# Cross-attention with a state-space layer: projections cut into pieces, maxima over two steps, sums on ScalarE, keys and values fetched per unit

## The chip, the cores and the metric

The kernel runs on one core of a Trainium2 chip, in float32. A core has five engines with queues of their own: TensorE (PE in the profile; its weight loads are shown apart as PEld), VectorE (DVE), ScalarE (ACT), GpSimd (POOL) and SyncE (SP, which here only issues transfers). Each works through its queue in order, and an instruction that waits holds up all that is behind it. PE writes to PSUM, a small memory of eight banks; DVE and ACT read it from there. The metric is the time on the device in microseconds; the median of runs is compared.

## The reference, cut to what matters

Of 4096 rows of width 512, each is normalized and attends to 3202 context rows with eight heads of 64; then follow a projection with a residual, a second normalization, a linear recurrence with a SiLU in it, and an output:

```python
x1  = x + mha(layernorm(x, g1, b1), layernorm(ctx, g1, b1))   # softmax(q k^T / 8) v, then W_o
u   = (layernorm(x1, g2, b2) @ W_in.T + b_in) @ Bmat          # 4096 x 64
s_t = silu(s_{t-1} @ A.T) + u_t                               # over 4096 positions
out = x1 + states @ Cmat + mean(program_probs) @ W_prog.T + b_prog
```

## The kernel before

There are three stages. The **preparation** normalizes the context, projects it to keys and values in 13 double chunks of 246 to 248 context rows, and stores them to DRAM (kd, vd). A list of side work (`side`, which ends with `queries(0, x0)`) is advanced between its chunks. The **attention loop** takes the rows in eight query blocks Q of 512. A block has eight units: four pairs of heads (hp) times two halves of 256 rows. A unit has 13 steps, one for each double chunk of keys. The **tail** finishes the last block's four tiles and runs the recurrence in sweeps (L831), writing the output.

In the loop the order on every engine is written out by hand, step by step (L718 to L768). The steps of one unit overlap with those of the next: in step g PE computes the scores of step g (L459), ACT copies them from PSUM to SBUF (L469), DVE keeps a running elementwise maximum (L480, one step later), and once a unit's scores are all there (16 steps after each), DVE subtracts the row maximum (L514), ACT takes the exponential (L524) and POOL adds the weights up (L533), and PE multiplies with the values (L542). The scores have two PSUM buffers of two banks each. The row maximum of a unit comes from `maximum`: PE transposes the running maximum (tt, L491), DVE reduces it (L498), PE spreads it over the keys (mb, L506).

Everything else is background work, held in generators that are advanced between the steps. `finish` ends a unit: the product is copied, POOL folds the sums of weights (L588), PE transposes them (pd, L594), DVE adds them up and takes the reciprocal (L599, L600), ACT widens it (L602), PE transposes it (rb, L607), DVE scales the result (L613). `project` ends a block, for each of its four tiles of 128 rows: PE's projection (pa, L627), DVE's residual (L636), the second normalization (`normalize`: statistics on DVE, L111 and L113, three small operations on POOL, L115 to L119, the scaling on ACT, L125), transposes (tp, L136), their copy (L652), the product pu (L659) and u (L663). `queries` prepares the next block: normalization, transposes, projection pq (L175), and ACT's bias (L184). In `background` (L704) two lists take turns: `first` holds the finishing of units, `rest` projections and queries. A generator says at each yield whether the next part needs PE results (True), and up to two parts of a list are advanced in a step. A whole projection of a tile, eight matrix instructions of 512 columns (float32 takes two instructions for one multiplication), is one such part:

```python
            for c in range(NC):
                nc.tensor.matmul(pa, o_t[Q, c][:, t * P : (t + 1) * P], wo[:, c, :], ...)
            yield True
```

The background shares two PSUM banks (`ps_m`), the maxima among them. Keys and values are fetched four steps ahead, on SP's queue, once for both halves of a pair (`load_k`, `load_v`, 13 buffers each); SP's queue also carries the fetches of x and the stores of x1. Outside the hand-written parts (the tail) a planner orders the instructions.

Of the kernel before, what the change touches and what calls it, by code (L numbers as in the profile page):

```python
# [18 lines left out]
P = 128  # L19
# [26 lines left out]
def xattn_ssm_kernel(  # L46
# [58 lines left out]
    ln = actx.enter_context(tc.tile_pool(name="ln", bufs=2))  # L105
# [25 lines left out]

    def transposes(pool, tag, xh, n, name):

        tp = pool.tile([P, NC, P], F32, tag=tag, name=f"tp_{name}")
        for c in range(NC):
            nc.tensor.transpose(  # L136
                tp[:, c, :n], xh[:n, c * P : (c + 1) * P], ident[:n, :n]
            )
        return tp[:, :, :n]

    xp_ = actx.enter_context(tc.tile_pool(name="xp", bufs=2))
    xnp = actx.enter_context(tc.tile_pool(name="xnp", bufs=2))
    qp = actx.enter_context(tc.tile_pool(name="qp", bufs=6))
    ps_m = actx.enter_context(tc.tile_pool(name="ps_m", bufs=2, space=PSUM))
    qt = {}

    def queries(Q, fetched=None):

        xns = []
        for half in range(2):  # L150
            xn = xnp.tile([P, NC, QU], F32, tag="xn", name=f"xn_{Q}_{half}")
            xns.append(xn)
            for t in range(NT // 2):
                r = Q * QB + half * QU + t * P
                if fetched:
                    xt = fetched[:, half * (NT // 2) + t, :]
                else:
                    xt = xp_.tile([P, H], F32, tag="x", name=f"x_{r}", bufs=3)
                    nc.sync.dma_start(xt, x[r : r + P, :])
                    yield False  # L160
                scaled = normalize(xt, P, f"x{r}", later=True)
                yield False
                yield False
                xh = scaled()
                yield False
                tp = transposes(ps_m, "m", xh, P, f"x{r}")
                yield True
                nc.scalar.copy(xn[:, :, t * P : (t + 1) * P], tp)
                yield False
                yield False  # L170
        for hp in range(NC):
            pq = ps_m.tile([P, 512], F32, tag="m", name=f"pq_{Q}_{hp}")
            for half in range(2):
                for i in range(NC):
                    nc.tensor.matmul(  # L175
                        pq[:, half * QU : (half + 1) * QU],
                        wq[:, i, hp * P : (hp + 1) * P],
                        xns[half][:, i, :],
                        start=(i == 0),
                        stop=(i == NC - 1),  # L180
                    )
            yield True
# [5 lines left out]
            yield False  # L188
# [22 lines left out]
    def shift(k):  # L211

        pr = ps_m.tile([P, 512], F32, tag="m", name=f"pr_{k}")
# [9 lines left out]
        pb = ps_m.tile([P, 512], F32, tag="m", name=f"pb_{k}")  # L223
# [15 lines left out]
    def side():  # L239
# [30 lines left out]
        pw = ps_m.tile([P, 512], F32, tag="m", name="pw")  # L270
# [8 lines left out]
        pt = ps_m.tile([P, NC, P], F32, tag="m", name="pt")  # L279
# [12 lines left out]
        pb = ps_m.tile([P, 512], F32, tag="m", name="pb")  # L292
# [16 lines left out]
        pm = ps_m.tile([P, 512], F32, tag="m", name="pm")  # L309
# [11 lines left out]
        for dst, terms in (  # L321
# [3 lines left out]
            pr = ps_m.tile([P, 512], F32, tag="m", name="pr")  # L325
# [126 lines left out]
    def scores(w, c):  # L452
# [3 lines left out]
        for b in range(2):  # L456
            for a in range(2):
# [3 lines left out]
                    kts[(*w["at"][:2], c)][r, b * n : (b + 1) * n],  # L461
# [20 lines left out]
    def maximum(w):  # L482

        m = small.tile([P, 2, 2], F32, tag="m", name=f"m_{w['name']}")
        tps = []
        for t in range(2):
            tp = ps_m.tile([P, 2, 2, CK], F32, tag="m", name=f"tt_{w['name']}_{t}")
            tps.append(tp)
# [7 lines left out]
        yield  # L496
        for t in range(2):
            nc.vector.tensor_reduce(  # L498
                m[:, t, :], tps[t].rearrange("p a b k -> p a (b k)"), AX.X, ALU.max
            )  # L500
        yield
        mb = ps_b.tile([P, 2, QU], F32, tag="b", name=f"mb_{w['name']}")
        w["mb"] = mb
        for t in range(2):
            for a in range(2):
# [4 lines left out]
                )  # L510

# [23 lines left out]
    def product(w, c):  # L535
# [4 lines left out]
        for b in range(2):  # L540
            for a in range(2):
                nc.tensor.matmul(  # L542
                    w["po"][a * HD : (a + 1) * HD, 0, :],
                    vts[(*w["at"][:2], c)][:n, b, a * HD : (a + 1) * HD],
# [34 lines left out]

# [388 lines left out]
```

## Time and profile before

| | us |
|---|---|
| median of 3 runs (2635.56 to 2644.17) | 2643.56 |
| profiled execution, its own time | 2643.8 |
| its span, first to last instruction | 2642.0 |
| preparation | 0 to 263 |
| attention loop | 263 to 2498 |
| tail | 2498 to 2642 |

| engine | busy us | share of the span | instructions |
|---|---|---|---|
| PE | 2498.9 | 95% | 16588 |
| PEld | 1422.2 | 54% | 16588 |
| DVE | 2144.1 | 81% | 2320 |
| ACT | 1837.8 | 70% | 2085 |
| POOL | 2066.3 | 78% | 1170 |

Rows of the profile name line, engine, operation, output<-input and count, then busy time in us, the mean of one in ns, and the idle time before them with what ended it. The ends of matrix instructions are modelled, so a busy PE need not be at its peak; starts are recorded, and the distance from one start to the next is the safer reading. The granted clock of TensorE is full in the loop (1.00) and lower in the tail (0.68).

### The profile page before, as it was taken

Reading aid. Unit: us, or ns where it says so; the run is one execution under the profiler, and the core shown is the slowest. Engines: PE = TensorE matmul, PEld = TensorE weight load, DVE = VectorE, ACT = ScalarE, POOL = GpSimd, SP = SyncE. Lnnn points to the kernel's source line nnn. Section 1 sums busy time; section 2 is a strip of 40 time slices with the busy share of each in tenths; the row PEclk is TensorE's granted clock in tenths of the full one; section 3 lists DMA queues with packets and bytes.
Section 4 is the critical chain, followed back from the end, with each engine's and each line's share of the span. In section 5 each row is a group of like instructions: output and inputs, shape, how many; then the busy total and the mean of one; then the engine's idle time right before and its main releaser. Section 6 shows DMA issues by size and latency. Waiting matters only on the chain.

```text
span 2642.0 us, 44166 instructions
## 1 busy us (share of the span) xinstructions
PE 2498.9 (95%) x16588; PEld 1422.2 (54%) x16588; DVE 2144.1 (81%) x2320; ACT 1837.8 (70%) x2085; POOL 2066.3 (78%) x1170
## 2 busy tenths in 40 slices
PE   7989899999999999999999999999999999999857
PEld 3445456555565555555655555555655555555433
DVE  2210897999979897999799988999799979999725
ACT  2232787877878787878787777778787878788510
POOL 1020497998979997999799988989799979999860
PEclk9999999999999999999999999999999999999966
DMA  3422221112212121222112211222121312221133
GB/s 124 138 87 73 74 68 49 51 57 84 59 45 62 50 83 32 58 65 68 45 54 68 67 56 51 57 84 59 43 62 49 86 30 60 64 58 54 60 112 128
DMA packets 164458, 176.62 MB, mean 67 GB/s; under 512 B 13480, under 2 KB 137424, under 8 KB 164242
## 3 DMA queue, kind: packets, MB, share of 16 engines
q1 hardware_dynamic: 155070, 157.68, 20.6%
q10 hardware_dynamic: 9172, 16.06, 1.8%
q8 instruction: 134, 2.20, 0.4%
q14 instruction: 82, 0.67, 0.1%
HBM read 143.81 MB, written 29.89 MB: 66 GB/s over the span
## 4 chain that ended last, share of the span: by engine, by line
PE 50%; DVE 27%; issue 11%; ACT 7%; POOL 2%; DMA 1%; SPq 1%; ACTq 0%; DVEq 0%; POOLq 0%
DVE top L480 17%; PE s L459 14%; PE po L542 12%; DVE p L514 5%; PE pq L175 4%; ACT p L469 4%; PE pa L627 4%; PE pv L388 3%; PE pk L414 3%; ACT p L524 2%; PE tt L491 2%; PE py_c L870 1%; DVE rd L599 1%; PE mb L506 1%; PE pu L659 1%
## 5 line engine op out<-in xcount | busy, mean ns | idle before, releaser
L533 POOL TENSOR_TENSOR acc<-p,acc 123x1024 f32<-123x1024 f32 x698 | 1658.7, 2376 | 112.2 <-ACT p L524 70.6
L469 ACT COPY p<-s 123x1024 f32<-123x1024 f32 (+1 forms) x832 | 834.9, 1004 | 274.6 <-PE s L459 261.9
L514 DVE TENSOR_TENSOR p<-p,mb 123x1024 f32<-123x1024 f32 (+1 forms) x832 | 1000.0, 1209 | 0.8 <-PE mb L506 0.8
L459 PE MATMUL s<-q,k 64*123 64x256 f32 (+1 forms) x6656 | 941.4, 402 | 61.2 <-DVE top L480 49.4
L524 ACT ACTIVATE p<-p 123x1024 f32<-123x1024 f32 (+1 forms) x832 | 880.2, 1058 | 141.2 <-DVE p L514 134.0
L480 DVE TENSOR_TENSOR top<-s,top 123x1024 f32<-123x1024 f32 x704 | 855.9, 1216 | 140.1 <-ACT p L469 132.2
L542 PE MATMUL po<-p,v 123*64 123x256 f32 (+1 forms) x6656 | 900.4, 392 | 1.1 <-ACT o L585 0.9
L459 PEld LDWEIGHTS s<-q,k 64*123 64x123 f32 (+1 forms) x6656 | 560.2, 182 | 374.3 <-DVE top L480 169.3
L542 PEld LDWEIGHTS po<-p,v 123*64 123x64 f32 (+1 forms) x6656 | 404.4, 136 | 399.0 <-issue 222.5
L533 POOL TENSOR_TENSOR acc<-p,p 124x1024 f32<-124x1024 f32 x64 | 152.0, 2376 | 161.2 <-ACT p L524 161.0
L627 PE MATMUL pa<-wo,o 128*128 128x512 f32 x256 | 119.6, 612 | 2.5 <-DVE x L636 2.5
L115 POOL TENSOR_SCALAR ve_c<-mv_c 123x1 f32<-123x1 f32 (+1 forms) x26 | 5.9, 228 | 146.9 <-DVE mv_c L113 116.7
L175 PE MATMUL pq<-xn,wq 128*128 128x256 f32 x512 | 117.9, 383 | 0.0
L358 DVE COPY ct<-tp_c 128x492 f32<-128x492 f32 (+1 forms) x13 | 8.7, 671 | 127.8 <-PE tp_c L136 127.8
L480 DVE TENSOR_TENSOR top<-s,p 124x1024 f32<-124x1024 f32 x64 | 77.7, 1214 | 38.7 <-DMA k<-kd 37.4
L175 PEld LDWEIGHTS pq<-xn,wq 128*128 128x128 f32 x512 | 94.8, 190 | 20.5 <-issue 6.3
L388 PE MATMUL pv<-wv,ct 128*123 128x512 f32 (+1 forms) x208 | 97.8, 615 | 0.0
L422 ACT ACTIVATE ks<-pk,bias 128x492 f32<-128x492 f32 (+2 forms) x28 | 18.0, 643 | 111.8 <-PE pk L414 63.6
L414 PE MATMUL pk<-ct,wk 128*128 128x492 f32 (+2 forms) x224 | 89.2, 550 | 0.0
L588 POOL TENSOR_TENSOR both<-acc 124x512 f32<-124x512 f32 x63 | 80.8, 1283 | 4.9
L627 PEld LDWEIGHTS pa<-wo,o 128*128 128x128 f32 x256 | 46.8, 192 | 62.5 <-issue 56.5
L498 DVE TENSOR_REDUCE m<-tt 128x2 f32<-128x496 f32 x128 | 79.7, 662 | 0.7 <-PE tt L491 0.7
(158 smaller groups left out, 1345.5 us busy)
## 6 DMA issues: line engine op xcount, KB each, us to landing
k<-kd SPq DMA_DIRECT2D x352, 123.0 KB
v<-vd SPq DMA_DIRECT2D x352, 123.0 KB
xr<-in_x_dram SPq DMA_DIRECT2D x32, 256.0 KB
out_dram<-row_c ACTq DMA_DIRECT2D x32, 256.0 KB
k<-kd SPq DMA_DIRECT2D x64, 124.0 KB
v<-vd SPq DMA_DIRECT2D x64, 124.0 KB
x<-in_x_dram SPq DMA_DIRECT2D x28, 256.0 KB
x1d<-x SPq DMA_DIRECT2D x28, 256.0 KB
```

The source lines that it names most:

```text
L175: nc.tensor.matmul(pq[:, half * QU : (half + 1) * QU], wq[:, i, hp * P : (hp + 1) * P], xns[half][:, i, :], start=(i == 0), stop=(i == NC ...
L388: nc.tensor.matmul(pv[:n, :H], ct[:, i, o : o + n], wv[:, i, :], start=(i == 0), stop=(i == NC - 1),)
L414: nc.tensor.matmul(pk[:, :n_g], wk[:, i, hp * P : (hp + 1) * P], ct[:, i, :n_g], start=(i == 0), stop=(i == NC - 1),)
L459: nc.tensor.matmul(s[:n, a, b, :], kts[(*w["at"][:2], c)][r, b * n : (b + 1) * n], q[r], start=True, stop=True,)
L469: nc.scalar.copy(t[:n], s[:n])
L480: nc.vector.tensor_tensor(w["top"][:n], s[:n], before[:n], ALU.max)
L514: nc.vector.tensor_tensor(t[:n], t[:n], w["mb"][:n].unsqueeze(2).to_broadcast([n, 2, 2, QU]), ALU.subtract,)
L524: nc.scalar.activation(t[:n], t[:n], AF.Exp)
L533: nc.gpsimd.tensor_tensor(w["acc"][:n], t[:n], before[:n], ALU.add)
L542: nc.tensor.matmul(w["po"][a * HD : (a + 1) * HD, 0, :], vts[(*w["at"][:2], c)][:n, b, a * HD : (a + 1) * HD], t[:n, a, b, :], start=(c == ...
L588: nc.gpsimd.tensor_tensor(both, acc[:, :, 0, :], acc[:, :, 1, :], ALU.add)
L627: nc.tensor.matmul(pa, o_t[Q, c][:, t * P : (t + 1) * P], wo[:, c, :], start=(c == 0), stop=(c == NC - 1),)
```

## The change

1. **Pieces of one feature chunk.** `project` and `queries` yield after every chunk c: a piece is the two instructions of one chunk. One piece goes at the end of a step (`tail`), after the product; steps in which a maximum has work get none. Parts on other engines go ahead of the scores (`heads`), at most one per generator and step. There are four generators: finish, two projections (a and b, every second tile each) and queries; the one with pieces under way owns the bank (`owner`). The queries' projection takes 512 columns at once instead of twice 256.
2. **Maxima over two steps.** tt and its reduction are done for one half of the columns, then for the other, in one bank (`ps_f`), which the finishing shares; the other background work has the other bank (`ps_m`).
3. **Statistics and sums on ScalarE.** In the loop the normalization's sum and sum of squares, the sums of weights and u move from DVE to ACT.
4. **Fetches per unit.** Keys and values are fetched for every unit, into 6 and 9 buffers instead of 13 each.
5. The last block's tiles keep DVE's statistics and get five PSUM banks of their own; x tiles, transposed queries and normalization buffers change in number, and the preparation takes the two banks in turns.

The diff, cut to its core:

```diff
+    def normalized(xt, name, got):
+        xh = ln.tile([P, H], F32, tag="xh", name=f"xh_{name}")
+        total = ln.tile([P, 1], F32, tag="total", name=f"total_{name}")
+        nc.scalar.activation(xh, xt, AF.Identity, accum_out=total)
+        yield "head"
+        mean = ln.tile([P, 1], F32, tag="mean", name=f"mean_{name}")
+        nc.gpsimd.tensor_scalar(mean, total, -1.0 / H, None, ALU.mult)
+        yield "head"
+        yield "head"
+        square = ln.tile([P, 1], F32, tag="square", name=f"square_{name}")
+        nc.scalar.activation(xh, xt, AF.Square, bias=mean, accum_out=square)
+        yield "head"
+        nc.gpsimd.tensor_scalar(ve, square, 1.0 / H, EPS, ALU.mult, ALU.add)
+        nc.gpsimd.tensor_tensor(rstd, ve, neg_half, ALU.pow)
+        nc.gpsimd.tensor_tensor(nmr, mean, rstd, ALU.mult)
+        yield "head"
+        yield "head"
+        nc.scalar.activation(xh, xt, AF.Identity, bias=nmr, scale=rstd)
+        got.append(xh)
...
# queries
+            pq = bank(name) if fetched else ps_m.tile([P, 512], F32, tag="m", name=name)
+            for i in range(NC):
+                nc.tensor.matmul(
+                    pq,
+                    wq[:, i, hp * P : (hp + 1) * P],
+                    xn[:, i, :],
...
+                if i < NC - 1 and not fetched:
+                    yield "pe"
+            yield "head"
...
# maximum
         for t in range(2):
-            tp = ps_m.tile([P, 2, 2, CK], F32, tag="m", name=f"tt_{w['name']}_{t}")
+            tp = ps_f.tile([P, 2, 2, CK], F32, tag="m", name=f"tt_{w['name']}_{t}")
...
-        yield
-        for t in range(2):
+            yield
             nc.vector.tensor_reduce(
-                m[:, t, :], tps[t].rearrange("p a b k -> p a (b k)"), AX.X, ALU.max
-            )
-        yield
+                m[:, t, :], tp.rearrange("p a b k -> p a (b k)"), AX.X, ALU.max
+            )
+            yield
...
# finish
-        nc.vector.tensor_reduce(rd, pd, AX.X, ALU.add)
+        for t in range(2):
+            for a in range(2):
+                nc.scalar.activation(
+                    junk, pd[:, t, a, :], AF.Identity, accum_out=rd[:, t, a : a + 1]
+                )
+        yield "head"
...
# project
+                if c < NC - 1:
+                    yield "pe"
+            yield "head"
             x1 = xp.tile([P, H], F32, tag="x1", name=f"x1_{r}")
             nc.vector.tensor_tensor(x1, pa, xt, ALU.add)
...
+                nc.sync.dma_start(x1d[r : r + P, :], x1)
+                yield from normalized(x1, f"y{r}", got)
...
-            nc.vector.tensor_scalar(
+            nc.scalar.activation(
                 u[hs, :, c0 : c0 + P // L].rearrange("s j c -> s c j"),
                 pu[hs].rearrange("s (c j) -> s c j", j=L),
-                bu[hs],
-                None,
-                ALU.add,
-            )
+                AF.Identity,
+                bias=bu[hs],
+            )
...
-        if half == 0:
-            t = kp.tile([P, 2 * CK], F32, tag="k", name=f"k_{Q}_{hp}_{c}")
+        t = kp.tile([P, 2 * CK], F32, tag="k", name=f"k_{i}_{c}", bufs=AHEAD + 2)
...
+        t = kp.tile([CK, 2, P], F32, tag="v", name=f"v_{i}_{c}", bufs=AHEAD + 5)
...
+    def advance(k, what):
+        if not beside[k] or waits.get(k, "head") != what:
+            return False
+        waits[k] = next(beside[k][0], None)
+        if waits[k] is None:
+            beside[k].pop(0)
+            waits.pop(k)
+        return True
+    def heads():
+        for k in beside:
+            if advance(k, "head") and owner == [k]:
+                owner.clear()
+    def tail():
+        if advance("finish", "pe"):
+            return
+        for k in owner or ("a", "b", "queries"):
+            if advance(k, "pe"):
+                owner[:] = [k]
+                break
...
# a step of the loop
+            for k in (2, 3):
+                if k in ends:
+                    next(ends[k]["max"])
             if exp:
                 weights(*exp)
+            heads()
             if now:
                 scores(*now)
...
-                    first.append(finish(mul[0]))
+                    beside["finish"].append(finish(mul[0]))
+                    waits["finish"] = "head"
+                    advance("finish", "head")
...
-            background(more=1 not in ends)
-            if 1 in ends:
-                ends[1]["max"] = maximum(ends[1])
-                next(ends[1]["max"])
+            for k in (1, 2, 3):
+                if k in ends:
+                    w = ends[k]
+                    if k == 1:
+                        w["max"] = maximum(w)
+                    next(w["max"])
+            if not ends:
+                tail()
...
+    ps_t = lastx.enter_context(tc.tile_pool(name="ps_t", bufs=5, space=PSUM))
+    tails = [project(NQB - 1, (t,), (tp_, NT, NT, ps_t)) for t in range(NT)]
```

## The prediction

> **What bounds the kernel now.** I read the share of each engine first, then the busy time by stretch, because the average hides three stages with different limits.
>
> ```profile
> 0.00:263.00 263.00, 233.97 (x706) 115.58 (x706) 46.27 (x106) 66.57 (x106) 32.87 (x97) 0.99 0.33 105
> 263.00:2498.00 2235.00, 2166.71 (x15630) 1258.84 (x15632) 2045.41 (x2085) 1754.64 (x1931) 1980.26 (x1021) 1.00 0.20 58
> 2498.00:2642.00 144.00, 98.27 (x256) 47.80 (x252) 52.46 (x129) 16.58 (x48) 53.22 (x52) 0.68 0.42 134
> ...
> 825.00:1106.00 281.00, 274.80 (x1972) 159.78 (x1968) 256.89 (x265) 220.81 (x245) 251.23 (x133) 1.00 0.21 59
> ```
>
> The columns are PE, PEld, DVE, ACT and POOL busy. The attention loop is 2235 of 2642 us. Inside it one query block of 512 rows (104 steps) takes 281 us: PE is busy for 274.8, DVE 256.9, POOL 251.2, ACT 220.8. A clean stretch, one unit of 13 steps without background work, looks different:
>
> ```profile
> 1044.79:1075.71 30.92, 29.84 (x227) 16.90 (x227) 30.69 (x31) 26.15 (x29) 29.76 (x14) 1.00 0.28 79
> ```
>
> There DVE is busy for 30.69 of 30.92 us, so DVE sets the pace. Whether PE is really full elsewhere I take from start times in the timeline of PE, since ends are modelled:
>
> ```profile
> 893.47 3.70 PE L627 MATMUL pa<-wo,o 128*128 128x512 f32 x8
> 897.10 1.13 PE L459 MATMUL s<-q,k 64*123 64x256 f32 x8
> 898.16 1.08 PE L542 MATMUL po<-p,v 123*64 123x256 f32 x8
> 899.17 1.13 PE L459 MATMUL s<-q,k 64*123 64x256 f32 x8
> ...
> 1073.12 1.13 PE L459 MATMUL s<-q,k 64*123 64x256 f32 x8 [0.29 <-DVE top L480]
> 1074.18 1.08 PE L542 MATMUL po<-p,v 123*64 123x256 f32 x8
> 1075.71 1.13 PE L459 MATMUL s<-q,k 64*123 64x256 f32 x8 [0.45 <-DVE top L480]
> ```
>
> From start to start, scores take 1.06 us and a product 1.015, so a step of PE alone is 2.075 us. A step that waits for the running maximum (1073.12 to 1075.71) is 2.59, and the steps after it 2.26. From 844 to 960 us PE never waits. So PE bounds the steps with projections, and DVE the others.
>
> **The ledger of one block.** By the same start-to-start reading: 104 steps x 2.075 = 215.8; maxima (tt) 8 x 0.995 = 8.0; mb and pd 16 x 0.575 = 9.2; rb 8 x 0.37 = 3.0; input transposes 8 x 0.58 = 4.6; pu 4 x 0.865 = 3.5; pa 4 x 3.63 = 14.5; pq 14.5. The sum is 273.0. The period is 280.8 (pa at 844.58 and 1125.37), so PE waits 7.8 us a block. That is all that relief of DVE can give: 7.8 x 6 middle blocks, about 47 us, plus the ends.
>
> **Pieces of projections.** The arithmetic stays: eight instructions of 512 columns at 0.432 us, 3.45 in all. But pa takes 3.63, and the groups of two and four transposes show the same excess (rb 0.37 for 2 x 0.108, pd 0.575 for 4 x 0.108): each change of group costs about 0.15 to 0.18. A piece of two instructions is therefore 0.863 + 0.175 = 1.04, four are 4.15. Per block: pa 16.6 instead of 14.5, pq 16.6 instead of 14.5. The Trainium skill, TensorE: Matmul & The Clock Gate, "Step-by-step: what each phase is for", says that weight loads are pulled ahead of running matmuls where row groups don't conflict or a background buffer takes them; by it a change of group would be free, four pieces would be 3.45 and a block 2.1 us cheaper than now rather than 4.2 dearer. The row decides, and the same page ("What overlaps and what doesn't") gives a reason: the overlap is seen only where row groups differ[...]. I take +4.2.
>
> **Maxima over two steps.** tt splits into two groups of four, so one more change of group per unit: 8 x 0.15 = +1.2. There is now one bank, and the order is tighter: the second half's reduction comes one step later, after a subtraction and a running maximum, and mb stands behind it on PE with the next scores queued behind mb. Counted from the end of the first tt half in a PE-bound stretch, PE reaches mb at 2.65 + 2.075 = 4.7 us; DVE's reduction (0.6), two subtractions (2.26), a maximum (1.13) and the second reduction (0.6) end at 4.6. It fits by 0.1, and DVE's own wait for the first half costs some 0.3 per unit. The PE floor of a block becomes 273.0 + 4.2 + 1.2 = 278.4.
>
> **Statistics and sums to ScalarE.** DVE loses what these rows show:
>
> ```profile
> L599 DVE TENSOR_REDUCE rd<-pd 128x4 f32<-128x496 f32 x63 | 42.0, 667 | 1.6 <-PE pd L594 1.6
> L111 DVE BATCH_NORM_STATS2 st_y<-x 128x6 f32<-128x512 f32 x32 | 22.2, 695 | 1.1
> L585 ACT COPY o<-po 128x256 f32<-128x256 f32 x63 | 23.5, 373 | 0.0
> L125 ACT ACTIVATE xh_x<-x,nmr_x,rstd_x 128x512 f32<-128x512 f32 x32 | 26.2, 820 | 0.0
> ```
>
> Neighbours overlap by 0.09, so 0.58 x 8 for rd, about 0.8 x 8 for the statistics (aggregate included; in the first block two tiles in a unit make 32.6 us of 30.9) and 0.35 x 4 for u: 12.4 us a block, 244 left. ACT gains per tile two passes of 512 (between 0.60, the plain copy, and 0.82): about 0.62 + 0.72 less overlap, x 8 = 9.2; four sums of 124 elements per unit, each 0.265 by the slope between 256 elements (0.373) and 1024 (1.003); u 1.5. No row has an accumulator output. Below I allow nothing, above 0.25 us for the read-out; VectorE: DVE Perf Modes, "Two Vector instructions with no wait between them", describes an accumulator output as a second instruction on DVE. I take 0.1, the order of the smallest ACT gap, which makes about 48 x 0.1 = 5. ACT is then 220.8 + 9.2 + 8.5 + 1.5 + 5 = 245 of 281: not the bound. Its new work stands before the copy of the scores, which PE needs two steps later. In the timeline that copy ends at 302.69 and the buffer is refilled at 304.15: 1.46 us of cover. Four sums are 4 x (0.265 + 0.1) = 1.46: just hidden. POOL gets one small scaling per tile, 0.25 x 8 = 2, and is 253.
>
> **Keys and values per unit.** SP issues two loads in every step instead of in half of the units: 0.34 + 0.25 us of its queue out of 2.7. The rate in the loading units was already this, with PE waiting on keys only in the ramp (3.9 us). A load follows the scores two steps back and is used four steps later, over 8 us. Behind a store of x1 the next key load is at most two steps late and still lands. Cost 0; without that lead, each late load would stop PE for its landing.
>
> **Sum.** A middle block keeps waits: about three clean units (free slots are 64, pieces 44) where DVE needs 30.69 - 0.58 + 0.3 = 30.4 against a PE unit of 29.65, 2.2 in all, and an estimated 0.5 elsewhere. 278.4 + 2.7 = 281.1 against 280.8: +0.3 x 6 = +2. The first block has no output projection and is DVE-bound: four tiles' statistics -3.2, six sums -3.4, pq +2.1: -4.5. The last has five clean units, 5 x -0.5, against pieces +2.5: 0. POOL holds these runs: twelve additions at 2.44 and one of 1.3 are 30.6 a unit. In the tail (2498 to 2545) the four last tiles pass one x1 buffer and POOL's chain, both unchanged; with five banks three pu no longer follow the last one (2540.6 to 2544.5): -4. Preparation: the same instructions with queries earlier, PE idle only about 10 us after its start: 0, within 4. Total -6.5. The profiled execution's own time is 2643.8 (span 2642.0 and 1.8 around it), level with the median 2643.56: 2637, say **2638**.
>
> **Rivals.** (1) **Waits vanish**: the pieces fill exactly the steps where DVE was late. For it: DVE has 37 us of slack a block. Against: pieces are drawn from a queue that runs dry around the fifth unit. Then a block is 278.4, -14 in six, the ends -7, the tail -6: 2617. With free group changes as well about 2595. (2) **The accumulator burst**: the four sums and their read-outs (L599's successor) exceed the 1.46 us before the copy of scores, so PE stands at the next scores. It decides from a read-out of 0.1 us; at 0.2 the excess is 0.4 x 63 units = 25, giving 2663; at 0.25, 2676. For it: ACT had idle time exactly ahead of that copy (262 us waiting for scores), now spent; against: 1.9 us of cover in PE-bound stretches. (3) **Nothing moves**: relief and dearer pieces cancel. That is the forecast within its error, not a separate case.
>
> **From cases to numbers.** Forecast 0.42 (own range 2627 to 2652), first rival 0.22, second 0.36. A measurement tells 0.3% or 8 us. The forecast splits 0.14 faster, 0.22 same, 0.06 slower; the first rival is faster; the second 0.34 slower, 0.02 same. So faster 0.36, same 0.24, slower 0.40. The 8-in-10 range takes most of both rivals: 2612 to 2676.
>
> **What would show it.** Right: pa in pieces 1.04 us start to start, PE's time per block near 279, DVE near 244, ACT near 245, waits of scores on the running maximum down from 49.4 us, a block period of 281. Wrong if the pieces cost 0.86; if scores wait for ACT's copy after the sums; if mb waits for the second reduction; or if the tail, whose order a planner sets, moves by more than 10 us.

## The result: slower, 2707 us against 2643

The changed kernel takes **2706.72 us** (median of 5 runs, 2705.46 to 2709.63), the one before 2643.32 (5 runs). The ratio is **1.0251, with a 95% interval of 1.0234 to 1.0268**: 2.5% slower, where 2638 was forecast and 2676 was the end of the range.

The first view of the profile after is the busy time by stretch (columns: length, then PE, PEld, DVE, ACT, POOL busy, granted clock, DMA share, GB/s). The first three stretches are preparation, loop and tail, the fourth a unit without pieces, the fifth a middle block.

```profile
0.00:270.00 270.00, 236.81 (x676) 111.08 (x677) 46.12 (x106) 66.91 (x106) 33.00 (x97) 0.97 0.33 103
270.00:2561.00 2291.00, 2207.90 (x15392) 1200.14 (x15394) 1974.59 (x1882) 1921.82 (x2686) 1982.92 (x1077) 1.00 0.35 102
2561.00:2707.00 146.00, 90.94 (x270) 45.28 (x265) 49.84 (x125) 18.99 (x53) 54.34 (x53) 0.71 0.40 132
1116.80:1148.70 31.90, 29.98 (x228) 16.88 (x226) 29.88 (x30) 27.37 (x37) 28.54 (x14) 1.00 0.36 104
1148.70:1436.76 288.06, 280.12 (x1939) 151.54 (x1937) 247.49 (x237) 242.95 (x345) 251.63 (x141) 1.00 0.36 103
```

The work moved as forecast: in a block DVE is busy for 247 us and ACT for 243 (244 and 245 were forecast). Both have slack, and yet a block takes 288.1 us instead of 280.8. Even the unit without pieces, which was to become shorter, went from 30.92 to 31.90, and DVE, 30.69 of 30.92 before, is now 29.88 of 31.90: it waits.

By the starts of the first scores and of the last product, the preparation went from 263.3 to 269.9 us (+6.6), the loop from 2231.8 to 2289.7 (+57.9), the rest from 146.9 to 147.2 (+0.3). The loop is the whole story but for a tenth.

What the pieces cost can be read in PE's timeline (start, then duration, both us):

```profile
939.55 1.12 PE L667 MATMUL pa<-wo,o 128*128 128x512 f32 x2
940.61 1.13 PE L494 MATMUL s<-q,k 64*123 64x256 f32 x8
...
950.94 1.12 PE L667 MATMUL pa<-wo,o 128*128 128x512 f32 x2
951.99 1.13 PE L494 MATMUL s<-q,k 64*123 64x256 f32 x8
```

From start to start a piece takes 1.05 to 1.06 us. PE's own time can be summed in this way: for each pair of neighbouring groups the shortest distance from start to start, times their number. In a middle block it is 278.8 us, against 272.5 before by the same reading: +6.3, where +5.4 was forecast. The rest of the period is PE standing: **9.4 us a block, where 8.4 were before and 2.7 were forecast**. Scores waiting for the maximum hold 4.6 of it (1.3 of these behind rb), transposes of the queries 2.3 and pu 1.8. Before, nearly all of it (7.2) was scores waiting for the maximum. So that wait did shrink, but new ones came beside it, and the two left the sum a little above the old one.

The timeline of ACT, DVE and PE in the unit without pieces shows the new wait (in brackets: idle time before, and what ended it):

```profile
1128.32 1.13 PE L494 MATMUL s<-q,k 64*123 64x256 f32 x8
...
1128.83 1.06 ACT L557 ACTIVATE p<-p 123x1024 f32<-123x1024 f32 x1 [0.30 <-DVE p L547]
...
1129.79 0.26 ACT L637 ACTIVATE wide<-pd 128x124 f32<-128x124 f32 x1
...
1129.94 0.19 ACT L637 ACTIVATION_READ_ACCUMULATOR wide<-pd 128x1 f32 x1
...
1131.13 0.19 ACT L637 ACTIVATION_READ_ACCUMULATOR wide<-pd 128x1 f32 x1
1131.22 1.00 ACT L504 COPY p<-s 123x1024 f32<-123x1024 f32 x1
...
1132.26 1.23 DVE L515 TENSOR_TENSOR top<-s,top 123x1024 f32<-123x1024 f32 x1 [1.21 <-ACT p L504]
...
1133.54 1.13 PE L494 MATMUL s<-q,k 64*123 64x256 f32 x8 [1.00 <-DVE top L515]
```

Four sums with their read-outs stand between the exponential (1128.83) and the copy of the scores that PE began at 1128.32: 1129.79 to 1131.22, 1.43 us. The copy ends at 1132.22, and only then, at 1132.26, does DVE's running maximum of *the same scores* begin. The buffer comes free when the maximum ends, and PE stands for 1.00 us. So the chain is copy, then maximum, then the scores two steps later. In the list of waits (us in total, times, longest) DVE's wait for the copy has more than doubled. Before and after:

```profile
DVE top L480 <- ACT p L469: 133.5, 114, 3.8
...
PE s L459 <- DVE top L480: 49.4, 99, 1.1
```

```profile
DVE top L515 <- ACT p L504: 301.7, 454, 34.5
...
PE s L494 <- DVE top L515: 45.0, 64, 1.5
...
PE pu L701 <- ACT xn L695: 11.2, 7, 1.6
```

One wait of 34.5 us at the start of the loop is in the 301.7; a like one before (37.4) is listed there under the first load of keys.

That a maximum starts only after the copy of its own scores has ended, although both only read, holds in the traces of both kernels: each of the 768 maxima starts at least 0.03 us after the end of its copy. The Trainium skill, PSUM — Partial Sum Buffer, "PSUM bank collisions raise a hardware error", gives a reason: two engines must not touch one bank in the same partitions at once, two reads included, so such accesses are put one after the other. The trace agrees: in the rows above, 0.04 us lie between the end of the one and the start of the other.

### The profile page after: what moved, and what is told of

It is laid out like the page before. It is cut to its first block, busy times and chain, and to the rows that moved or that the text cites. A ratio compares the mean times of both kernels' runs of the same rounds, so it can differ in the third digit from the quotient of the medians.

```text
span 2706.8 us, 46074 instructions
## 1 busy us (share of the span) xinstructions
PE 2535.6 (94%) x16332; PEld 1356.5 (50%) x16332; DVE 2070.5 (76%) x2113; ACT 2007.7 (74%) x2845; POOL 2070.3 (76%) x1226
## 4 chain that ended last, share of the span: by engine, by line
PE 69%; ACT 12%; DVE 11%; issue 4%; POOL 2%; DMA 1%; SPq 1%; ACTq 0%; POOLq 0%; DVEq 0%
PE s L494 23%; PE po L575 21%; DVE top L515 8%; PE pq L209 5%; ACT p L504 5%; PE pa L667 4%; PE pv L423 4%; PE pk L449 3%; PE tt L524 3%; ACT p L557 2%; DVE p L547 2%; ACT wide L637 2%; PE mb L538 1%; POOL row_c L838 1%; PE py_c L927 1%
## 5 line engine op out<-in xcount | busy, mean ns | idle before, releaser
L209 PE MATMUL pq<-xn,wq 128*128 128x512 f32 x256 | 140.5, 638 | 1.2 <-ACT xn L203 1.2
L667 PE MATMUL pa<-wo,o 128*128 128x512 f32 x256 | 140.0, 638 | 0.0
L530 DVE TENSOR_REDUCE m<-tt 128x2 f32<-128x496 f32 x128 | 85.4, 667 | 35.2 <-PE tt L524 34.4
L524 PE MATMUL tt<-ident,top 124*128 124x124 f32 x512 | 82.3, 283 | 3.1 <-DVE top L515 1.6
L524 PEld LDWEIGHTS tt<-ident,top 124*128 124x128 f32 x512 | 52.9, 141 | 53.2 <-issue 20.0
```

Of the source, the lines that this page charges most:

```text
L209: nc.tensor.matmul(pq, wq[:, i, hp * P : (hp + 1) * P], xn[:, i, :], start=(i == 0), stop=(i == NC - 1),)
L524: nc.tensor.transpose(tp[:, a, b, :], w["top"][:, a, b, t * P : (t + 1) * P], ident[:CK, :CK],)
```

## Experiments

None of these kernels leaves work out. Loop times (first scores to last product) are from the one trace of each kernel. They leave out the preparation, which varied by about 4 us, and the tail, which varied between 138 and 150, in kernels whose edit touches neither. Two theories stood against each other at first: **A**, ScalarE's parts ahead of the scores' copy hold up the chain; **C**, the pieces' and half maxima's own starts on PE make the loss. **B** was that PE stands too close behind ScalarE at transposes and pu.

| kernel | median us | ratio to before, 95% interval | loop us |
|---|---|---|---|
| before | 2636 to 2643 (by group of runs) | 1 | 2231.8 |
| changed | 2706.7 | 1.0251 (1.0234 to 1.0268) | 2289.7 |
| changed, sums on DVE | 2677.4 | 1.0137 (1.0112 to 1.0163) | 2261.5 |
| changed, finishing behind the copy | 2680.7 | 1.0143 (1.0119 to 1.0166) | 2263.4 |
| changed, statistics on DVE | 2710.4 | 1.0260 (1.0238 to 1.0283) | 2290.9 |
| changed, more room | 2714.9 | 1.0272 (1.0248 to 1.0295) | 2296.5 |
| changed, whole projections | 2719.6 | 1.0291 (1.0261 to 1.0320) | 2312.5 |
| changed, whole, finishing behind | 2679.9 | 1.0144 (1.0123 to 1.0164) | 2271.5 |
| changed, finishing behind, bank paused | 2674.0 | 1.0138 (1.0110 to 1.0166) | 2258.0 |
| changed, all remedies | 2643.8 | 1.0010 (1.0000 to 1.0019) | 2236.8 |
| changed, maximum from SBUF | 3182.5 | 1.2044 (1.2021 to 1.2068) | 2763.1 |
| before, maximum from SBUF | 3240.3 | 1.2269 (1.2240 to 1.2297) | 2825.5 |
| before, sums on ACT, first form | 2679.9 | 1.0147 (1.0130 to 1.0164) | 2273.0 |
| before, sums on ACT, second form | 2693.0 | 1.0187 (1.0164 to 1.0210) | 2277.8 |
| before, sums on ACT, third form | 2647.2 | 1.0038 (1.0023 to 1.0053) | 2238.0 |
| before, queries' statistics on ACT | **2628.5** | **0.9949** (0.9933 to 0.9966) | 2224.0 |
| before, both (second form) | 2678.7 | 1.0143 (1.0123 to 1.0163) | 2271.6 |
| before, both (third form) | 2656.3 | 1.0076 (1.0057 to 1.0095) | 2248.8 |
| before, half maxima | 2648.5 | 1.0048 (1.0030 to 1.0065) | 2242.6 |
| before, fetch per unit | 2639.6 | 1.0005 (0.9996 to 1.0015) | 2232.0 |

### Is it the burst ahead of the copy?

Sums back on DVE:

```diff
-        for t in range(2):
-            for a in range(2):
-                nc.scalar.activation(
-                    junk, pd[:, t, a, :], AF.Identity, accum_out=rd[:, t, a : a + 1]
-                )
+        nc.vector.tensor_reduce(rd, pd, AX.X, ALU.add)
```

> The changed kernel with the four sums of weights back on DVE as one reduction; all else as changed. Theory A (ScalarE's parts ahead of the copy of the scores hold up the running maximum and with it PE's next scores): the 1.5 us burst goes, the clean unit falls from 31.9 to about 30.6 us, and of the 3.3 us a block that scores wait for the maximum some 2 go: 20 to 30 us less than 2707, 2677 to 2687. Theory B (transposes and pu placed one step too close to ScalarE's work): no more than 5 us. Theory C (the pieces' and half maxima's own starts, 5.4 us a block, make the loss): no more than 5 us; DVE, given back 4.6 us a block, is still below PE.

The same instructions, but the finishing's parts on other engines (the sums, the widening, the scaling) behind the copy of the scores:

```diff
 def heads():
-        for k in beside:
+        for k in ("a", "b", "queries"):
...
             if now:
                 scores(*now)
+            advance("finish", "head")
```

> The changed kernel with the finishing's parts on other engines (the sums, the widening, the scaling) issued behind the copy of the scores instead of ahead of it; same instructions. Theory A: the order alone makes the loss at the ends of units, so this gains as much as taking the sums away, 20 to 30 us (2677 to 2687), and the copy follows the scores without a gap. Rival: the price is ScalarE's time itself (about 50 us more of it in the loop than was forecast by the rows) or PE's pieces: no change beyond 5 us, or slower, as the exponential behind the burst is now late.

Each takes back about 1.1% of the 2.5%, 28.2 and 26.3 us of the loop; the block falls from 288.1 to 284.4 and 284.7. In the second kernel nothing was removed: **the place of the finishing's parts in the queues, not their amount, makes nearly half of the loss**. The unit without pieces falls to 31.1 and 31.0, not to 30.6: the sums were not all of it. Theory A holds for this half.

Unit by unit, the sums' way to PE is only in part the one that theory A names. The pieces are spread over the units alike in these two kernels and the changed one. In four of the eight units of a block PE hardly stands in any of the three: there the burst is hidden. In two others (the unit without pieces, and the one with two transposes of queries) scores wait less for the maximum with the sums gone, 1.5 us a block. In the last two, 2.2 us a block, it is the transposes and pu that wait less for ScalarE, which stood behind the same sums with its reading of u and its copy of the transposes.

### The statistics, and the room before transposes

Statistics back on DVE, in as many steps (`normalized` calls `normalize(..., later=True)`):

> The changed kernel with the normalization's statistics in the loop back on DVE (as before the change), the same number of parts between them. Theory A: two passes per tile no longer stand ahead of a copy; with scores' waits of 3.3 us a block shared between sums and statistics, 5 to 12 us less than 2707. Theory B: the scaling stays as close to the transposes as it was, so the 2.3 us a block that they wait remain. Rival (DVE's relief is what the changed order lives on): DVE gets 6.4 us a block back, and units without pieces, already set by DVE and ScalarE, are longer: 5 to 15 us slower than 2707.

No change (loop +1.2). In this kernel the move of the statistics neither costs nor gains: whether the passes on ScalarE cost nothing and DVE's relief of 6.4 us a block brings nothing, or the two cancel, this run doesn't tell.

```diff
                 yield from normalized(xt, name, got)
+                yield "head"
                 yield "pe"
...
                 yield from normalized(x1, f"y{r}", got)
+                yield "head"
             yield "pe"
...
             nc.scalar.copy(xn, tp)
+            if not pools:
+                yield "head"
             yield "pe"
```

> The changed kernel with one more step between the normalization's scaling and the transposes, and one more between the copy of the transposes and pu. Theory B: PE no longer waits for ScalarE at these places, 2.3 + 1.8 = 4.1 us a block, 7 blocks: 25 to 30 us less than 2707, near 2680. Theory A or C alone: no change beyond 5 us, since PE would then wait for the next scores instead, at the same moment.

A miss: not faster, the loop 6.8 us longer. Who is waited for before the transposes of queries (us and times, PE and its weight loads counted together) tells why:

```profile
  ACT xn L697: 37.7, 24
  ACT xh_x L125: 28.0, 4
```

The first line is the new one (the second is of the preparation): with more room, PE comes to the transposes while ScalarE has still to read the *previous* content of the one background bank. A later attempt gave room before the transposes and paused the bank as well, on top of the late finishing (neither is shown again):

```diff
             nc.scalar.copy(xn, tp)
+            hold[:] = [True]
...
 def tail():
+        if hold:
+            hold.clear()
+            return
```

> The changed kernel with the finishing behind the copy (2681 alone), one more step between the normalization's scaling and the transposes, and no new piece in the step in which ScalarE starts to read the transposes out of the one bank. More room alone had lost 8 us, as the next piece then stood for ScalarE's read of that bank. If the stands at transposes and pu (1.4 + 0.9 us a block after the late finishing) are the bank's, both go: 12 to 18 us less, about 2665. If they only pass on to the next scores, or the left-out steps push pieces into other units: within 5 us of 2681.

The stand at pu went (0.9 us a block to none), as did one at rb (0.8), and that at transposes of queries fell from 1.4 to 1.0; but scores, and the maxima's transposes, waited 0.6 more each for the running maximum. The ratio is within its interval of the late finishing's: more than half of the stands pass on. By itself B is not the cause. Room and pause have a side effect: they delay the queries' pieces, so that five of them fall into a block's last unit, and no unit without pieces is left.

### Are the pieces the cause?

```diff
                     stop=(c == NC - 1),
                 )
-                if c < NC - 1:
-                    yield "pe"
```

and likewise in `queries`.

> The changed kernel with both projections in one piece of eight instructions again (no step between the chunks). Theory C (each extra change of group costs 0.17 us): 24 changes a block go, 4.2 us; in seven blocks that is 29 us, so 2678, if the waits stay. Theory A on top: 24 steps a block now have no piece to hide ScalarE's burst behind, up to 1 us a unit in about two more units a block, so half of it comes back: 2685 to 2692. Rival (pieces are what lets VectorE keep up): 2707 or more.

> The changed kernel with whole projections and the finishing's parts behind the copy. With the burst out of the way, the 4.2 us a block of the pieces' changes of group should come back almost whole: 284.5 falls to 281 or 282, 15 to 25 us less than the 2681 of the late finishing alone. Rival (whole projections empty the steps in which ScalarE and VectorE catch up, whatever the burst): 2681 or more, as with the burst, where whole projections cost 13 us.

As to the pieces, theory C falls; the half maxima stayed in. Whole projections do save PE's own time (278.8 to 274.0 us a block), but waits rise from 9.4 to 17.3: the units without pieces are now three, at 32.07 each. With the finishing behind the copy they are 31.19, and whole projections are level in time with pieces (loop 8.1 longer, ratio the same). The pieces cost about what was forecast for them, and more than pay for it: the waits that return without them are larger.

### Cutting the chain at the maximum

If the maximum read ScalarE's copy in SBUF, the scores' buffer would be free one maximum earlier:

```diff
-        nc.vector.tensor_tensor(w["top"][:n], s[:n], before[:n], ALU.max)
+        nc.vector.tensor_tensor(w["top"][:n], w["s"][c][:n], before[:n], ALU.max)
```

> The kernel before with the running maximum taken from ScalarE's copy in SBUF instead of from the scores in PSUM, and nothing else. The maximum now starts only after the copy in any case, so the scores' buffer comes free about 1.1 us earlier. If the chain scores, copy, maximum, scores sets the steps without pieces: the 6.9 us a block that scores wait for the maximum go in part and VectorE may fall behind and catch up, 10 to 40 us less than 2641. Rival (VectorE's own 30.7 us of work set those units): within 5 us. If reading SBUF twice is slower for VectorE beside POOL: slower by 0.1 us or more for each of 800 maxima, 80 us.

> The changed kernel with the same single edit: the running maximum read from the copy in SBUF. Theory A: the burst ahead of the copy then has 1.1 us more of cover, so the 3.3 us a block of waits for the maximum go, and the clean unit falls from 31.9 to below 31: 20 to 35 us less than 2707. Rival (the burst delays by ScalarE's own occupancy, not by the chain over the maximum): within 5 us.

Both lost 20% and more, so they say nothing of the chain. The groups of DVE and of POOL in the first of the two:

```profile
L480 DVE TENSOR_TENSOR top<-p,top 123x1024 f32<-123x1024 f32 x704 | 1396.8, 1984 | 155.7 <-ACT p L469 152.9
...
L533 POOL TENSOR_TENSOR acc<-p,acc 123x1024 f32<-123x1024 f32 x698 | 2052.7, 2941 | 177.7 <-ACT p L524 123.0 <-POOL acc L533 0.4
```

A maximum takes 1.98 us instead of 1.22, and at the same time POOL's addition 2.94 instead of 2.38. The Trainium skill, SBUF — State Buffer, "Who interferes with whom", says that a DVE instruction with two inputs in SBUF contends with GpSimd's reads, and one with at most one does not. Both rows agree, and so does the subtraction, which reads one operand from PSUM and stayed at 1.21. The same trace settles that it is the meeting with POOL and not SBUF as such: the 28 of these maxima during which POOL did nothing took 1.22 us, the 589 that lay (nine tenths or more) within POOL's work 2.11.

### One part at a time, in the kernel before

**Sums on ScalarE, behind the copy.** The first form put the sums and DVE's reciprocal in one step:

> The kernel before with the sums of weights on ScalarE, in the background behind the copy of the scores, and nothing else. Theory A (the place does the harm, not the move): VectorE is relieved of 0.58 us a unit where it sets the pace, about 0.4 us in half of 63 units, so 5 to 15 us less than 2641; the clean unit falls from 30.92 to about 30.5. Rival (the sums on ScalarE cost by themselves): 10 us or more slower than 2641.

```profile
1081.87 1.21 DVE L514 TENSOR_TENSOR p<-p,mb 123x1024 f32<-123x1024 f32 x1
1084.29 0.18 DVE L606 RECIPROCAL rd<-rd 128x4 f32<-128x4 f32 x1 [1.22 <-ACT wide L603]
1084.39 1.21 DVE L480 TENSOR_TENSOR top<-s,top 123x1024 f32<-123x1024 f32 x1
```

A new wait, of my own making: a reciprocal of 0.18 us holds DVE for 1.22 us, with the running maximum behind it. A step between was to remove it:

```diff
+        yield False
         nc.vector.reciprocal(rd, rd)
```

> The kernel before with the sums of weights on ScalarE behind the copy of the scores, and one step between them and VectorE's reciprocal, which in the first form stood 1.22 us a unit in VectorE's queue. Theory A (the place does the harm): VectorE sheds 0.58 us a unit, the clean unit falls from 30.92 to about 30.5, 2 us a block: 10 to 17 us less than 2641. Rival (1.5 us of ScalarE in one piece delays something wherever it stands, here the exponential behind it): 2641 or more.

> The kernel before with both: sums of weights and queries' statistics on ScalarE, behind the copy, with a step before VectorE's reciprocal. If the two gains are of different units they add: 22 to 35 us less than 2641, about 2612, faster than both kernels. If ScalarE's bursts meet in the units with statistics: no better than the better of the two.

The stand was still there (DVE's reciprocal waited for ScalarE 63 times, 88.3 us in all): in the kernel before, the background advances two parts in one step when the first needed a result of PE, so the extra yield was used up in the same step. These two runs say no more than the first form did. The third form has two yields:

> As the second form, but with two steps' ends between the sums and VectorE's reciprocal: in the second form both parts were still advanced in one step, and VectorE stood for the sums 63 times, 88.3 us in all. Theory D (that wait is the whole loss of the two forms before): it goes, VectorE sheds 0.58 us a unit, 10 to 17 us less than 2641. Theory E (ScalarE's burst of 1.6 us holds up the exponential or the next copy wherever it stands): 2650 or more, with scores waiting for the maximum by more than the 6.9 us a block of before.

> The kernel before with the queries' statistics on ScalarE (which alone gave 12 us) and the sums as in the third form. Theory D: the gains add, 22 to 30 us less than 2641. Theory E: slower than the statistics alone, 2640 or more.

The stand is gone from the list of waits, and with it 35 us of the loop's 41: so much of the loss of the first form was DVE's standing for its own reciprocal (theory D). But the loop is still 6.2 us longer than before, though DVE does 0.58 us less in each unit. DVE's wait for the scores' copy rose from 133.5 to 180.5 us: the relief became waiting. The unit without background work is 30.88 instead of 30.92, and two of the three units that hold output projections are 0.8 longer (38.98 for 38.20, 36.22 for 35.44). In each of these two, where PE never stood before, the transposes of the output's normalization now stand 0.4 us for ScalarE's scaling, those of the maximum 0.3 and scores 0.1 for the running maximum: the burst reaches PE by other ways. With the statistics added (17.0 longer) projections of the queries stand for ScalarE's sums as well (up to 1.6 us). Sums on ScalarE lose in each place that was tried.

**Queries' statistics on ScalarE**, four tiles a block, in the background behind the copy:

```diff
-                scaled = normalize(xt, P, f"x{r}", later=True)
-                yield False
-                yield False
-                xh = scaled()
...
+                nc.scalar.activation(xh, xt, AF.Identity, accum_out=total)
+                yield False
+                nc.gpsimd.tensor_scalar(mean, total, -1.0 / H, None, ALU.mult)
+                yield False
+                yield False
+                nc.scalar.activation(xh, xt, AF.Square, bias=mean, accum_out=square)
+                yield False
...
```

> The kernel before with only the queries' normalization statistics (four tiles a block) on ScalarE, in the background behind the copy. The ledger of before has 3.2 us a block of waits for the maximum in the two units that hold these statistics on VectorE (1.58 and 1.64). If VectorE's load is their cause: most of it goes, 2 to 3 us a block, 12 to 20 us less than 2641. If moving work to ScalarE gives it back as waits elsewhere: within 5 us.

**Faster than both kernels: 0.9949 (0.9933 to 0.9966), 12 us less than before.** In the changed kernel, moving eight tiles' statistics did nothing; here moving four pays. PE's stands for the running maximum fall from 7.7 to 5.5 us a block, and the block from 280.9 to 279.5. That DVE's relief makes the gain is likely but not shown, as the edit does a second thing: it has more yields, and with them the queries' tiles are spread over more units (one in each of four, where two units held two each), and their four projections all come into one. The same yields with the statistics left on DVE were not run.

**Half maxima and fetches:**

```diff
-        yield
-        for t in range(2):
+            yield
             nc.vector.tensor_reduce(m[:, t, :], tp..., AX.X, ALU.max)
+            yield
```

> The kernel before with the maxima over two steps, transposes and reduction for one half of the columns and then for the other, and nothing else. By the ledger: one more change of group per unit, 1.2 us a block, and VectorE's wait for the half transposes where it sets the pace, 0.3 us a unit: 8 to 20 us more than 2641. Rival (mb, tight by 0.1 us in the ledger, waits for the second reduction): 30 us or more. Rival (the two halves cost nothing, as nothing waits for them): within 5 us.

> The kernel before with keys and values fetched for every unit into 6 and 9 buffers, and nothing else. By the prediction's step: 0, within 3 us. Rival (twice the traffic delays stores and fetches of x, or PE waits for keys): 5 us or more above 2641.

The half maxima cost 10.8 us of loop, in the range of the ledger; the unit without pieces is 31.26 instead of 30.92, 0.17 of it between mb and the next scores. The fetches cost nothing (loop +0.2).

### All remedies at once

Sums on DVE, the finishing behind the copy, the room with the paused bank, and in the preparation the scaling of queries two parts later:

```diff
-                xh = normalize(fetched[:, t, :], P, name)
+                scaled = normalize(fetched[:, t, :], P, name, later=True)
+                yield "pe"
+                yield "pe"
+                xh = scaled()
                 yield "pe"
```

> The changed kernel with all of it: sums of weights back on VectorE, the finishing behind the copy, one more step before the transposes and a pause of the bank behind them, and the queries of the preparation scaled two parts later, so that PE does not stand 10.3 us for ScalarE there. Sums and place are one cause (29 and 26 us alone), so together no more than about 32; the bank 7; the preparation 6.6 by its stage: 2707 less 40 to 46, 2661 to 2667. If only the sum of weights counts: 2675. Kernel before: 2637; what stays above it is the half maxima (11 us alone) and the pieces' starts.

2643.8 us, **1.0010 (1.0000 to 1.0019) of the kernel before: the loss is gone** but for 5.0 us of the loop, which a shorter preparation and tail offset, though pieces, half maxima, the statistics and u on ScalarE, and the doubled fetches are all still there. It was 17 us better than the best of the expectation. Busy time by stretch, a middle block last:

```profile
261.00:2498.00 2237.00, 2203.47 (x15382) 1200.19 (x15383) 2004.69 (x1945) 1839.31 (x2182) 1980.12 (x1077) 1.00 0.36 105
...
1120.64:1401.33 280.69, 279.51 (x1939) 151.55 (x1937) 251.29 (x245) 232.39 (x281) 251.39 (x141) 1.00 0.37 106
```

and of its waits:

```profile
PE s L500 <- DVE top L521: 16.8, 35, 1.5
...
PE tp_x L160 <- ACT xh_x L125: 4.7, 4, 1.5
...
PE tp_x L160 <- ACT u L708: 1.5, 6, 0.3
```

PE stands for 2.0 us a block on top of its own 278.9, where 2.7 and 278.4 were forecast for the change; scores' waits for the maximum are 16.8 us in all, from 45.0. In the loop this kernel differs from the one with late finishing and paused bank in one thing, the sums, and they took another 21 us with them. So sums on DVE and sums in another place are *not* one cause, as I had expected: behind the copy the sums still delayed things (the third form shows the same). The block falls under 281 with the sums gone, the finishing late and the bank paused; the late finishing and the pause were not tried one by one with the sums gone, so what each of them gives there is not separated.

The preparation is 260.8 instead of 269.9 us. In the changed kernel PE stood there for the scaling of queries for 10.28 us; with two parts between it stands for 1.02 (second fence), as it did in the kernel before:

```profile
142.58 0.67 ACT L457 ACTIVATE ks<-pk,bias 128x492 f32<-128x492 f32 x1 [14.88 <-DMA kd<-ks]
143.15 0.80 ACT L125 ACTIVATE xh_x<-x,nmr_x,rstd_x 128x512 f32<-128x512 f32 x1
...
144.01 1.11 PE L160 MATMUL tp_x<-ident,xh_x 128*128 128x128 f32 x4 [10.28 <-ACT xh_x L125]
```

```profile
144.88 0.66 PE L160 MATMUL tp_x<-ident,xh_x 128*128 128x128 f32 x4 [1.02 <-ACT xh_x L125]
```

## Why the prediction was wrong, step by step

**Ledger of the block before: right** but for half a microsecond: 272.5 of PE's own and 8.4 of waits by exact starts, against 273.0 and 7.8.

**Pieces, +4.2 a block, and the half of tt, +1.2: right, a little low.** A piece takes 1.05 to 1.06 us against 1.04; PE's own time rose by 6.3 against 5.4, to 278.8 where 278.4 was forecast. The rule that weight loads are pulled ahead, by which changes of group would be free, was rightly set behind the row. (By the prediction's own figures it would have made a block 1.4 us cheaper, not 2.1: twice 14.5 less 4 x 3.45.) But the reason given for the row, that loads overlap only where row groups differ, does not fit the trace. Within a projection the next full-height load runs beside the running matrix instruction. In the group of the kernel before that begins at 893.47:

```profile
894.00 0.19 PEld L627 LDWEIGHTS pa<-wo,o 128*128 128x128 f32 x1 [0.24 <-issue]
...
897.10 0.18 PEld L459 LDWEIGHTS s<-q,k 64*123 64x123 f32 x2 [0.76 <-DVE p L514]
```

Only the first load of the next group comes no earlier than that group's first matrix instruction, which starts at 897.10 too. That this is the whole price of a change is not shown. That mb "fits by 0.1" was 0.17 us short in units without pieces; alone the half maxima cost 10.8 us.

**Statistics and sums to ScalarE: the busy times right, the cover wrong. This is the step that failed.** The four sums take 1.43 us where 1.46 was worked out (the read-out is an instruction of 0.196 us that overlaps its sum; 0.1 was my allowance for what it adds). But "that copy ends at 302.69 and the buffer is refilled at 304.15: 1.46 us of cover" took the copy for the last reader of the buffer. In the same stretch the maximum of the same scores stands between the two:

```profile
301.69 1.00 ACT L469 COPY p<-s 123x1024 f32<-123x1024 f32 x1
...
302.88 1.21 DVE L480 TENSOR_TENSOR top<-s,top 123x1024 f32<-123x1024 f32 x1
```

It starts 0.19 us after the copy's end and ends 0.06 us before the refill. The copy could come 0.19 us late there, not 1.46, before it held up the maximum, and 1.43 less 0.19 leaves 1.24; 1.00 us of stand was measured at the scores in the unit without pieces. The second path was not in the prediction at all: ScalarE's reading of u and its copy of the transposes, for which PE's transposes and pu wait, come late behind the same sums. The second rival named this burst and this victim, with "PE stands at the next scores", but hung it on the read-out. With the right cover it would have read 1.24 x 63 = 78 us. That would have overshot what the sums cost: taking them off ScalarE gave back 28 us of loop, since in half of the units PE does not stand for them. Its own "against", the cover in PE-bound stretches, is what those units show.

**Waits left, 2.7 a block: wrong, 9.4.** Over six blocks that is 6.7 x 6 = 40 us, the greater part of the loop's 58. The sum counted only DVE's load, in three units without pieces, as a source of waits; there is one such unit. Not counted were ScalarE's burst, the stands at transposes and pu (4.1 us a block: 2.9 of it for ScalarE's scaling and copy, 1.1 for its reading of u out of the one background bank) and 1.3 at the scores behind rb. The run with all remedies has the forecast block, 280.7 against 281.1: the ledger described that kernel, not the change as it orders ScalarE's queue. About half of the loop's loss is thus put down to the sums and their place by runs that changed these alone. The rest went only together with the paused bank and both remedies for the sums at once, and how it is shared among them stays open.

**First and last block, -4.5 and 0: wrong.** +7.7 and +6.3, from one first score of a block to the next; no run takes these two apart.

**Fetch per unit, 0: right**, +0.2 alone.

**Preparation, 0 within 4: wrong, +6.6.** "The same instructions with queries earlier" missed that PE now meets the transposes before ScalarE, held for 14.9 us by stores of keys, can scale; given two parts of room, the stage is as short as before. **Tail, -4: not seen**, +0.3; by its spread of 138 to 150 us in kernels that don't touch it, a gain of 4 couldn't be told.

**"Waits vanish": refuted** for this order of work. **"Nothing moves"** is what the parts gave in a better order.

## What to carry to other kernels

Count cover to the *last* reader of a buffer, and put every reader of one PSUM tile in a row, also where they are on different engines. A small operation put into an in-order queue ahead of the instruction that feeds the critical chain can cost most of its length (1.00 of 1.43 us here), and nothing where PE has work enough to cover it, so ask of each moved step what is queued behind it; the same instructions behind that point gave back 26 us. Before taking load off an engine, find the units where that engine sets the pace: four tiles' statistics taken off DVE, with their tiles spread over more units, won 0.5% in the kernel that DVE held up, and eight tiles' in the changed one nothing.

## What was unexpected of the hardware

An accumulator output on ScalarE is an instruction of its own: 196 ns, 252 times in the groups of the changed kernel, yet a sum of 124 elements with its read-out takes only about 0.36 to 0.39 us from start to start. A maximum with both inputs in SBUF took 1.98 us against 1.22 with one in PSUM, and slowed POOL from 2.38 to 2.94; where POOL was idle it took 1.22 as well. Nor had it been expected that all the sums' relief of DVE (0.58 us a unit) turns into waiting for the copy, even when the sums stand behind it.
